# Cross-attention on one core: the first query product in two banks, the mean copied ahead of rstd's transpose, x's second half loaded in two pieces, more identity transposes

## Chip, core and metric

The kernel runs on one core of one Trainium2 chip. The metric is device time in microseconds; lower is better. Every time below is from the profile of one execution or from the list of timed runs. In the profile PE is TensorE's matmul, PEld its weight load, DVE VectorE, ACT ScalarE, POOL GpSimd and SP SyncE, whose queue issues nearly all DMAs. L317 is line 317 of the kernel.

## What is computed

Cross-attention with a LayerNorm ahead of it and a residual behind it: 8 batches of 256 rows of 1024 numbers, 32 heads of 32, keys and values both taken straight from the context (256 rows for each batch).

```python
mu = jnp.mean(hidden_states, axis=-1, keepdims=True)
var = jnp.var(hidden_states, axis=-1, keepdims=True)
x = (hidden_states - mu) * jax.lax.rsqrt(var + LN_EPS) * ln_gamma + ln_beta
Q = _split_heads(x @ Wq.T)
K = _split_heads(memory_keys)
V = _split_heads(memory_values)
scores = jnp.einsum('bhsd,bhtd->bhst', Q, K) * scale
scores = jnp.where(mask, scores, -jnp.inf)
probs = jax.nn.softmax(scores, axis=-1)
attn = jnp.einsum('bhst,bhtd->bhsd', probs, V)
out = attn @ Wout.T
return residual + out
```

## The kernel before

The work is cut into 64 steps n: batch n // 8, and within it a group of four heads, which is one 128-column chunk of the query. For each step PE makes scores (L525), VectorE adds the mask's bias and takes a minimum (L563), ScalarE takes exponents (L567), GpSimd and others normalise (L582), VectorE transposes in blocks (L588), and PE multiplies by the values (L675). Output projections of the batch before run in between (L759). The order on each engine is the order of the program text: the schedule is written out by hand, and the framework only adds the waits that tiles need. A matmul in float32 is two passes in the profile, a transpose is one.

The change touches only the start-up, which treats batch 0 apart, so that the first scores do not wait for a whole LayerNorm. x of batch 0 is loaded in halves of 128 rows: s=1 first, in two pieces of 512 columns (`load_x`, L133), then s=0 in one piece. In program order:

- `keep_busy` (L121) issues transposes of an identity tile into a PSUM tile that nobody reads.
- `ln_stats` (L231 to L239): VectorE takes statistics of rows, GpSimd raises the variance to the power -0.5 (rstd).
- `transpose_x0` (L275): PE turns raw x into PSUM, four 128x128 blocks in a bank; there are two such banks.
- `spread` (L282): PE transposes the mean, and then rstd, broadcast over columns, so that each lies along the free dimension. Both go into one PSUM tile, `stat0`.
- `keep_mean` (L285) and `keep_rstd` (L301): ScalarE copies each to SBUF.
- `centre_x0` (L288): VectorE subtracts the mean while it takes the transposed x out of PSUM.
- `gammas` (L296 on ScalarE, L298 on VectorE): each of the eight chunks is multiplied by gamma. For s=1 all eight go to ScalarE, for s=0 four each.
- `first_q` (L317): the query product of step 0 on centred x that is not yet divided by its deviation. One bank holds 128 columns for s=0, 128 for s=1, and a column that gives the bias from beta.
- `take_bias` (L329), `take_q` (L325 on VectorE, L326 on ScalarE): the bias is copied; the product is multiplied by rstd, and the bias is added.
- `scale_x0` (L304): the normalised x for the other query chunks, on VectorE and GpSimd.
- `mask_bias` (L515): VectorE turns the mask into a number to add.

Then come the scores of s=1, and a first softmax in two parts, with the second and third query products (`make_q`, L380) between them. SP's queue holds, behind the loads of x, the first query weights, the keys, the mask, and then other weights.

Of the kernel before, what the change touches and what calls it, by code (L numbers as in the profile page):

```python
# [46 lines left out]
F32 = mybir.dt.float32  # L47
# [4 lines left out]
P = 128  # L52
# [7 lines left out]
def xattn_kernel(  # L60
# [11 lines left out]
    B, S, D = x.shape  # L72
# [30 lines left out]
    ps_v = ctx.enter_context(tc.tile_pool(name="ps_v", bufs=2, space=PS))  # L103
    ps_q = ctx.enter_context(tc.tile_pool(name="ps_q", bufs=1, space=PS))
# [14 lines left out]
    def keep_busy(times):  # L119
        for _ in range(times):  # L120
            nc.tensor.transpose(busy, ident, ident)  # L121

    keep_busy(6)


    xs, ks, vs, rs = {}, {}, {}, {}
# [1 line left out]
    def load_x(b, s, h=None):  # L128

        if b not in xs:  # L130
            xs[b] = xp.tile([P, NS, D], F32, tag="x", name=f"x_{b}")
        cols = ds(0, D) if h is None else ts(h, 512)
        nc.sync.dma_start(xs[b][:, s, cols], x[b, ts(s, P), cols])  # L133
# [25 lines left out]
    wq = const.tile([P, NC, NC, P], F32, tag="wq", name="wq")  # L159
# [9 lines left out]
    def load_wq(o):  # L169
        nc.sync.dma_start(wq[:, o], wq_[o])  # L170
# [26 lines left out]
    nc.scalar.dma_start(gb, gamma_beta)  # L197
    load_x(0, 1, 0)
    load_x(0, 1, 1)
    load_x(0, 0)  # L200
    load_wq(0)
    load_k(0)
    load_mask(0)
# [42 lines left out]
    def ln_norm(b, s, engine):  # L246
# [15 lines left out]
    xcT0, xnT0 = (  # L262
        lnp.tile([P, NC, S + 1], F32, tag="xnT", name=f"x{which}T_0") for which in ("c", "n")
    )
    xnTs[0] = lambda c: xnT0[:, c, :]
    rows = sums_x.rearrange("p i c a k -> p (i c a k)")
    rows0, means0 = rows[:, :S], rows[:, ds(S, S)]
    px0, stat0 = {}, {}

    def transpose_x0(s, g):  # L270

        px0[s, g] = ps_v.tile([P, NC // 2, P], F32, tag="pv", name=f"px0_{s}_{g}")
        for i in range(NC // 2):
            chunk = xs[0][:, s, ts(NC // 2 * g + i, P)]
            nc.tensor.transpose(px0[s, g][:, i, :], chunk, ident)  # L275

    def spread(s, what):

        if what == 0:
            stat0[s] = ps_o.tile([P, 2, P], F32, tag="po", name=f"stat0_{s}")  # L280
        one = mvs[0][:, s, 0:1] if what == 0 else rstds[0][:, s : s + 1]
        nc.tensor.transpose(stat0[s][:, what, :], one.to_broadcast([P, P]), ident)  # L282

    def keep_mean(s):
        nc.scalar.copy(means0[:, ts(s, P)], stat0[s][:, 0, :])  # L285

    def centre_x0(s, g):
        nc.vector.tensor_tensor(  # L288
            xcT0[:, ts(g, NC // 2), ts(s, P)], px0[s, g],
            means0[:, ts(s, P)].unsqueeze(1).to_broadcast([P, NC // 2, P]), ALU.subtract,  # L290
        )
# [8 lines left out]
    def keep_rstd(s):  # L300
        nc.scalar.copy(rows0[:, ts(s, P)], stat0[s][:, 1, :])  # L301

    def scale_x0(s, g, engine):
        engine.tensor_tensor(  # L304
            xnT0[:, ts(g, NC // 2), ts(s, P)], xcT0[:, ts(g, NC // 2), ts(s, P)],
            rows0[:, ts(s, P)].unsqueeze(1).to_broadcast([P, NC // 2, P]), ALU.mult,
        )

    QUERY_0 = (0, 1, 2, 3, 4, 6, 5, 7)

    def first_q(s, chunks=QUERY_0):

        if s == 1 and chunks[0] == 0:
            pqs[0] = ps_q.tile([P, 512], F32, tag="pq", name="pq_0")
        cols = ds(0, P) if s == 0 else ds(P, P + 1)
        for c in chunks:
            nc.tensor.matmul(  # L317
                pqs[0][:, cols], wq[:, 0, c, :], xcT0[:, c, cols],
                start=(c == 0), stop=(c == NC - 1),
            )  # L320

    def take_q(o, bank, cols):

        to = qa[:, o, cols]
        nc.vector.tensor_tensor(to, bank[:, cols], rows0[:, cols], ALU.mult)  # L325
        nc.scalar.activation(to, to, AF.Identity, bias=qa[:, o, S : S + 1])  # L326

    def take_bias(o, bank):
        nc.scalar.copy(qa[:, o, S : S + 1], bank[:, S : S + 1])  # L329
# [39 lines left out]
    to_move, pqs = {}, {}  # L369
# [147 lines left out]
    def scores(n, part=range(NS)):  # L517
        if n not in scs:
            scs[n] = [
                ps_s.tile([P, NS, T], F32, tag="sc", name=f"sc_{n}_{j}") for j in range(NH)  # L520
            ]
        for s in part:
            for j in range(NH):
                r = slice(j * HD, (j + 1) * HD)
                nc.tensor.matmul(  # L525
                    scs[n][j][:, s, :], qa[r, n % NQ, ts(s, P)], ks[n - n % 2][r, n % 2, :],
                    start=True, stop=True,
                )
# [389 lines left out]
    def gammas(s):  # L918
        for c in QUERY_0:
            gamma_x0(s, c, nc.vector if s == 0 and c in (2, 4, 6, 7) else nc.scalar)  # L920
# [5 lines left out]
    transpose_x0(1, 0)  # L926
    keep_busy(2)
    transpose_x0(1, 1)
    keep_busy(2)
    spread(1, 0)  # L930
    keep_busy(3)
    spread(1, 1)
    keep_busy(3)
    keep_mean(1)
    keep_rstd(1)
    centre_x0(1, 0)
    centre_x0(1, 1)
    gammas(1)
# [2 lines left out]
    scale_x0(1, 1, nc.gpsimd)  # L941
    transpose_x0(0, 0)
    transpose_x0(0, 1)
    first_q(1, QUERY_0[:5])
    spread(0, 0)
    first_q(1, QUERY_0[5:])
    spread(0, 1)
    keep_mean(0)
    centre_x0(0, 0)
    centre_x0(0, 1)  # L950
    take_bias(0, pqs[0])
    gammas(0)
    keep_rstd(0)
    take_q(0, pqs[0], slice(P, S))
    scale_x0(0, 0, nc.vector)
    scale_x0(0, 1, nc.gpsimd)
    mask_bias(0)
    first_q(0)
    scores(0, (1,))
    take_q(0, pqs[0], slice(0, P))  # L960
    first = softmax_parts(0, (partial(copy_q, 1), partial(copy_q, 2)), (), (), {}, [
        partial(ln_stats, 1, 0), partial(ln_stats, 1, 1),
        partial(ln_norm, 1, 0, nc.vector),
# [34 lines left out]
    for n in range(N):  # L998
# [117 lines left out]
        if N - NQ + 2 < n < N - 1:  # L1116

            c = n - (N - NQ + 3)
# [104 lines left out]
```

## Time and profile before

| | before |
|---|---|
| median of 3 runs | 574.05 us (573.84 to 575.56) |
| profiled execution, whole | 575.86 us |
| its span, first to last instruction | 574.0 us |
| mean granted TensorE clock | 0.994 |
| busy: DVE | 468.3 us (82%) |
| busy: ACT | 426.3 us (74%) |
| moved by DMA | 119.02 MB, mean 207 GB/s |

A row of a timeline gives the start, the length from the first start to the last end, the engine, the line, the operation, what is written and read, the count, and in brackets the idle time just before it with what ended that. The chain of waits goes back from the last instruction, at each step to what released it. In rows of windows, each engine's busy time comes with the number of its instructions; the granted clock is 1.00 at full speed. A row of DMA issues ends with the median time from issue to landing.

### The profile page before, as it was taken

What the parts mean: (1) busy time and instruction counts of PE and PEld (TensorE: products, weight loads), DVE (VectorE), ACT (ScalarE), POOL (GpSimd) and SP (SyncE); (2) the same over time, 40 slices, a digit from 0 to 9 for tenths busy, and PEclk for the clock granted to TensorE, in tenths of its full rate; (3) what the DMA queues carried; (4) which work ended last, traced back from release to release, by engine and by line L of the source; (5) the groups of instructions that cost most, each with busy time, mean ns of one, the idle gap of its engine ahead of it and who ended that gap; (6) DMA issues with size and microseconds to landing.
All of it is one profiled execution on the core that took longest, in us unless ns stands there. A gap on an engine that the chain in (4) does not pass through costs nothing.

```text
span 574.0 us, 20189 instructions
## 1 busy us (share of the span) xinstructions
PE 563.7 (98%) x7246; PEld 394.3 (69%) x7246; DVE 468.3 (82%) x1718; ACT 426.3 (74%) x1478; POOL 397.9 (69%) x639
## 2 busy tenths in 40 slices
PE   6999999999999999999999999999999999999997
PEld 5777887677666776677676677667766777755544
DVE  4789889999897888988889788988878768778823
ACT  4489989998676876688577877778767766768920
POOL 3498897899875764975658675686657667448780
PEclk9799999999999999999999999999999999999999
DMA  8936477874878876886679767786667865536751
GB/s 304 397 104 197 150 207 231 265 233 122 248 254 241 236 203 188 250 245 201 175 213 284 195 199 228 221 253 199 196 175 226 243 197 142 139 104 178 218 160 73
DMA packets 47219, 119.02 MB, mean 207 GB/s; under 512 B 8976, under 2 KB 9744, under 8 KB 47120
## 3 DMA queue, kind: packets, MB, share of 16 engines
q1 hardware_dynamic: 46976, 117.74, 68.7%
q8 instruction: 57, 0.93, 0.7%
q14 instruction: 42, 0.34, 0.2%
q10 hardware_dynamic: 144, 0.01, 0.0%
HBM read 66.33 MB, written 11.53 MB: 136 GB/s over the span
## 4 chain that ended last, share of the span: by engine, by line
PE 90%; DMA 3%; DVE 3%; ACT 1%; POOL 1%; SPq 1%; issue 1%; DVEq 0%; POOLq 0%; ACTq 0%
PE po_S L759 19%; PE pq_A L486 18%; PE pv L675 11%; PE sc L525 11%; PE po_A L759 9%; PE pq L380 8%; PE pq_S L486 7%; PE po_end L826 3%; PE po_last L826 1%; DMA r<-in_x_dram 1%; ACT e L567 1%; PE pq L317 1%; DVE e L563 1%; DMA pT<-pT 1%; POOL e L582 1%
## 5 line engine op out<-in xcount | busy, mean ns | idle before, releaser
L582 POOL TENSOR_SCALAR e<-e,rden 128x256 f32<-128x256 f32 x466 | 216.7, 483 | 126.3 <-DVE rden L574 124.1
L567 ACT ACTIVATE e<-e,mn 128x256 f32<-128x256 f32 x512 | 254.1, 502 | 45.9 <-DVE mn L563 44.8
L588 DVE STREAM_TRANSPOSE pT<-e 128x512 f32<-128x512 f32 x256 | 178.9, 704 | 37.8 <-POOL e L582 32.8
L563 DVE CUSTOM_DVE_ANT_0 e<-sc,mb 128x256 f32<-128x256 f32 x512 | 185.3, 416 | 26.5 <-PE sc L525 26.3
L594 ACT COPY pc<-pT 128x512 f32<-128x512 f32 x128 | 79.0, 617 | 57.3 <-DVE pT L588 35.4
L567 ACT ACTIVATION_READ_ACCUMULATOR e<-e,mn 128x1 f32 x512 | 98.4, 192 | 0.0
L525 PEld LDWEIGHTS sc<-k,qa 32*128 32x128 f32 x1024 | 46.5, 185 | 42.1 <-issue 21.6
L525 PE MATMUL sc<-k,qa 32*128 32x256 f32 x1024 | 74.3, 403 | 0.0
L759 PE MATMUL po_S<-wo,at 128*128 128x512 f32 x152 | 74.3, 606 | 0.0
L675 PE MATMUL pv<-pT,v 64*32 64x128 f32 x4096 | 74.2, 274 | 0.0
L675 PEld LDWEIGHTS pv<-pT,v 64*32 64x32 f32 x4096 | 57.0, 105 | 22.5 <-issue 9.8
L759 PE MATMUL po_A<-wo,at 128*128 128x512 f32 x128 | 59.4, 605 | 0.0
L380 PE MATMUL pq<-xnT,wq 128*128 128x256 f32 (+1 forms) x240 | 55.6, 386 | 1.0 <-ACT qa L389 1.0
L486 PEld LDWEIGHTS pq_A<-xnT,wq 128*128 128x128 f32 x416 | 48.5, 192 | 6.2 <-issue 5.0
L380 PEld LDWEIGHTS pq<-xnT,wq 128*128 128x128 f32 x240 | 44.9, 191 | 10.0 <-issue 2.2
L759 PE MATMUL po_S<-wo,s 128*128 128x512 f32 x104 | 50.2, 607 | 0.9 <-DVE r L801 0.9
L486 PE MATMUL pq_A<-xnT,wq 128*128 128x128 f32 x416 | 48.5, 275 | 0.0
L574 DVE RECIPROCAL rden<-den 128x2 f32<-128x2 f32 x256 | 38.2, 149 | 6.6 <-ACT e L567 4.8
L563 DVE DVE_READ_ACCUMULATOR2_ANT mn<- 128x1 f32 x512 | 42.7, 83 | 0.0
L759 PEld LDWEIGHTS po_A<-wo,at 128*128 128x128 f32 x128 | 22.9, 189 | 25.7 <-issue 24.7
L759 PEld LDWEIGHTS po_S<-wo,at 128*128 128x128 f32 x152 | 25.5, 190 | 19.5 <-issue 19.5
L792 POOL TENSOR_TENSOR r<-r,p 128x512 f32<-128x512 f32 x24 | 30.6, 1277 | 4.4 <-DMA r<-in_x_dram 4.2
(109 smaller groups left out, 675.5 us busy)
## 6 DMA issues: line engine op xcount, KB each, us to landing
v<-in_kv_dram SPq DMA_DIRECT2D x32, 512.0 KB, 4.3
pT<-pT SPq DMA_DIRECT2D x128, 128.0 KB, 2.7
pT<-pc SPq DMA_DIRECT2D x128, 128.0 KB, 4.1
ring<-kept_T SPq DMA_DIRECT2D x20, 512.0 KB, 4.7
k<-in_kv_dram SPq DMA_DIRECT2D x32, 256.0 KB, 3.7
x<-in_x_dram SPq DMA_DIRECT2D x15, 512.0 KB, 6.0
r<-in_x_dram SPq DMA_DIRECT2D x28, 256.0 KB, 4.5
out_dram<-r SPq DMA_DIRECT2D x28, 256.0 KB, 4.0
```

Source lines behind the costliest of these rows:

```text
L380: nc.tensor.matmul(pqs[n], wq[:, o, c, :], xnTs[b](c), start=(c == 0), stop=(c == NC - 1),)
L486: nc.tensor.matmul(pqs[b][:, o, :], w[:, c], x_[:, c], start=begins and o + c == 0, stop=c == NK - 1, skip_group_check=True,)
L525: nc.tensor.matmul(scs[n][j][:, s, :], qa[r, n % NQ, ts(s, P)], ks[n - n % 2][r, n % 2, :], start=True, stop=True,)
L563: nc.vector.tensor_tensor_reduce(out=e[:, s, :], in0=pss[j][:, s, :], in1=mbs[n // NQ], scale=1.0, scalar=NO_SCORE, op0=ALU.add, op1=ALU.m ...
L567: nc.scalar.activation(e[:, s, :], e[:, s, :], AF.Exp, bias=mn[:, s : s + 1], scale=-1.0, accum_out=den[:, s : s + 1],)
L574: nc.vector.reciprocal(rden, dens[j])
L582: engine.tensor_scalar(es[j][:, s, :], es[j][:, s, :], rden[:, s : s + 1], 1.0, ALU.mult, ALU.mult,)
L588: nc.vector.transpose(pT[:, :, :, j, :, :].rearrange("p a i s k -> p (a i) s k"), es[j].rearrange("p s (b t) -> p b s t", t=K),)
L594: nc.scalar.copy(pc[:, :, ts(j, 2)], pT[:, 1, :, ts(j, 2)])
L675: nc.tensor.matmul(pvs[n][r][j * HD : (j + 1) * HD], vs[n - n % 2][ts(r, 2 * K), i, ds(n % 2 * P + j * HD, HD)], pT[ts(r, 2 * K), :, i, j, ...
L759: nc.tensor.matmul(po, operand(b, name)[:, c], wo[:, which, c], start=begins and c == 0, stop=c == NK - 1, skip_group_check=not begins,)
L792: nc.gpsimd.tensor_tensor(r, r, p1s[b], ALU.add)
```

## The change

- There are 14 identity transposes at the very start instead of 6. Two ahead of the first `spread` are gone; 4 instead of 3 follow the mean's and rstd's `spread` of s=1 (the latter now behind `keep_rstd`); 3 new ones stand behind `keep_rstd` of s=0.
- x's rows of s=0 are loaded in two pieces of 512 columns.
- `keep_mean` stands ahead of rstd's `spread`, for s=1 and for s=0. `keep_rstd` follows that `spread` directly; for s=0 it is ahead of the centring and the gamma products now. `take_bias` stands between the two centrings.
- Six chunks of the s=1 product stand ahead of the mean's `spread` of s=0, instead of five.
- The s=0 half of `first_q` has a bank of its own, from the pool with the two banks that `transpose_x0` used.

```diff
-    keep_busy(6)
+    keep_busy(14)
...
     load_x(0, 1, 0)
     load_x(0, 1, 1)
-    load_x(0, 0)
+    load_x(0, 0, 0)
+    load_x(0, 0, 1)
     load_wq(0)
...
-    px0, stat0 = {}, {}
+    px0, stat0, halves_q0 = {}, {}, {}
...
     def first_q(s, chunks=QUERY_0):
 
-        if s == 1 and chunks[0] == 0:
-            pqs[0] = ps_q.tile([P, 512], F32, tag="pq", name="pq_0")
+        if chunks[0] == 0:
+            pool, tag = (ps_q, "pq") if s == 1 else (ps_v, "pv")
+            halves_q0[s] = pool.tile([P, 512], F32, tag=tag, name=f"pq_0_{s}")
         cols = ds(0, P) if s == 0 else ds(P, P + 1)
         for c in chunks:
             nc.tensor.matmul(
-                pqs[0][:, cols], wq[:, 0, c, :], xcT0[:, c, cols],
+                halves_q0[s][:, cols], wq[:, 0, c, :], xcT0[:, c, cols],
                 start=(c == 0), stop=(c == NC - 1),
             )
...
     transpose_x0(1, 1)
-    keep_busy(2)
     spread(1, 0)
-    keep_busy(3)
+    keep_mean(1)
+    keep_busy(4)
     spread(1, 1)
-    keep_busy(3)
-    keep_mean(1)
     keep_rstd(1)
+    keep_busy(4)
     centre_x0(1, 0)
     centre_x0(1, 1)
...
-    first_q(1, QUERY_0[:5])
+    first_q(1, QUERY_0[:6])
     spread(0, 0)
-    first_q(1, QUERY_0[5:])
+    keep_mean(0)
+    first_q(1, QUERY_0[6:])
     spread(0, 1)
-    keep_mean(0)
+    keep_rstd(0)
+    keep_busy(3)
     centre_x0(0, 0)
+    take_bias(0, halves_q0[1])
     centre_x0(0, 1)
-    take_bias(0, pqs[0])
     gammas(0)
-    keep_rstd(0)
-    take_q(0, pqs[0], slice(P, S))
+    take_q(0, halves_q0[1], slice(P, S))
     scale_x0(0, 0, nc.vector)
     scale_x0(0, 1, nc.gpsimd)
     mask_bias(0)
     first_q(0)
     scores(0, (1,))
-    take_q(0, pqs[0], slice(0, P))
+    take_q(0, halves_q0[0], slice(0, P))
```

## The prediction

> **What bounds the kernel now.** I read the busy shares first, then the chain of waits, then windows with the granted clock, then the timelines of single engines over the first 22 us, where every edit lies.
>
> ```profile
> PE 563.7 (98%) x7246; PEld 394.3 (69%) x7246; DVE 468.3 (82%) x1718; ACT 426.3 (74%) x1478; POOL 397.9 (69%) x639
> ```
>
> TensorE (PE) fills 98% of the span, so what the change can win is a start-up that ends earlier. The chain of waits (start, length, what) shows it:
>
> ```profile
> 9.73 1.12 PE pq L317 x10
> ...
> 12.29 0.75 DVE xcT L288 x2
> ...
> 14.71 3.75 PE pq L317 x16
> 18.46 1.20 PE sc L525 x8
> 19.66 0.41 DVE e L563
> ...
> 22.81 0.35 DVE e L563
> ...
> 30.36 0.41 DVE e L563
> ...
> 36.04 3.75 PE pq L380 x16
> ```
>
> Up to 12.29 row means are made; there the centring of x's first 128 rows starts (s=0; the second 128 rows, s=1, go first). At 14.71 the sixteen passes of the last half query product run at 3.75/16 = 0.234 us each; ten passes of the same line took 1.12/10 = 0.112. From 19.66 to 36 the chain is VectorE, ScalarE and GpSimd work of the first softmax, and then PE. No load is on it there, so I let what is won at 19.66 pass to the end in full.
>
> The clock explains the 0.234. Windows (busy of PE, PEld, DVE, ACT, POOL; granted clock; DMA share; GB/s), and below them PE alone, cut at the changes of clock and halfway between:
>
> ```profile
> 13.50:14.00 0.50, 0.00 (x0) 0.00 (x0) 0.50 (x4) 0.50 (x3) 0.00 (x0) 0.83 1.05 426
> ...
> 20.50:21.00 0.50, 0.50 (x3) 0.23 (x1) 0.50 (x3) 0.50 (x3) 0.00 (x0) 0.84 1.03 410
> ```
>
> ```profile
> 0.17:3.59 3.42, 1.59 (x7) 1.00 0.48 146
> 3.59:7.00 3.41, 3.41 (x15) 1.00 0.93 308
> 7.00:10.42 3.42, 2.66 (x23) 1.00 0.92 343
> 10.42:13.83 3.41, 1.53 (x12) 1.00 1.02 415
> 13.83:17.24 3.41, 2.54 (x12) 0.50 1.03 408
> 17.24:20.66 3.42, 3.42 (x17) 0.50 1.03 410
> ```
>
> A clock of 0.83 in a slice is full speed for two thirds of it, so the clock fell at 13.83; likewise it came back at 20.66. It fell after a window with 1.53 us of work (45%), stayed low after 2.54 us (74%), rose after a full one, and was kept at 2.66 us (78%). The column says 1.00 from the start; spacing says otherwise:
>
> ```profile
> 1.35 1.54 PE L121 MATMUL busy<-ring 128*128 128x128 f32 x6 [1.35 <-POOL ring masks.py:199]
> 3.54 1.12 PE L275 MATMUL px<-ring,x 128*128 128x128 f32 x4 [0.65 <-DMA x<-in_x_dram]
> ...
> 6.58 0.42 PE L121 MATMUL busy<-ring 128*128 128x128 f32 x1
> ...
> 7.23 0.49 PE L121 MATMUL busy<-ring 128*128 128x128 f32 x3
> 10.68 0.27 PE L282 MATMUL stat<-ring,mv 128*128 128x128 f32 x1
> 11.63 0.32 PE L282 MATMUL stat<-ring,rstd 128*128 128x128 f32 x1
> 14.71 3.75 PE L317 MATMUL pq<-xcT,wq 128*128 128x128 f32 x16 [2.75 <-DVE qa L325]
> ...
> 21.15 0.71 PE L525 MATMUL sc<-k,qa 32*128 32x256 f32 x8
> 21.79 6.35 PE L380 MATMUL pq<-xnT,wq 128*128 128x257 f32 x28
> ```
>
> Six identity transposes start (1.54-0.42)/5 = 0.22 us apart, three at 7.23 (0.49-0.27)/2 = 0.11 apart: PE was at half speed until about 7.0.
>
> **The change, part by part.** *Two banks.* The row at 14.71 waited 2.75 us for VectorE to read the other half out of the shared bank. With its own bank the s=0 half waits only for its scaled chunks. The rows that feed it:
>
> ```profile
> 5.74 0.21 DVE L234 BATCH_NORM_AGGREGATE mv<-st 128x2 f32<-128x12 f32 x1
> ...
> 8.94 1.27 DVE L231 BATCH_NORM_STATS2 st<-x 128x6 f32<-128x512 f32 x2
> 10.24 0.21 DVE L234 BATCH_NORM_AGGREGATE mv<-st 128x2 f32<-128x12 f32 x1
> ...
> 13.49 0.87 DVE L298 TENSOR_SCALAR xcT<-xcT,gs 128x128 f32<-128x128 f32 x4
> 14.27 0.28 DVE L325 TENSOR_TENSOR qa<-pq,sx 128x128 f32<-128x128 f32 x1
> 14.47 0.69 DVE L304 TENSOR_TENSOR xnT<-xcT,sx 128x512 f32<-128x512 f32 x1
> 15.08 1.27 DVE L515 TENSOR_SCALAR mb<-mk 128x256 f32<-128x256 uint8 x1
> ```
>
> ```profile
> 7.43 0.27 ACT L285 COPY sx<-stat 128x128 f32<-128x128 f32 x1 [5.21 <-PE stat L282]
> ...
> 8.52 2.45 ACT L296 ACTIVATE xcT<-xcT,gs 128x128 f32<-128x128 f32 x8 [0.66 <-DVE xcT L288]
> 11.99 0.27 ACT L285 COPY sx<-stat 128x128 f32<-128x128 f32 x1 [1.02 <-PE stat L282]
> ...
> 13.01 1.28 ACT L296 ACTIVATE xcT<-xcT,gs 128x128 f32<-128x128 f32 x4 [0.70 <-DVE xcT L288]
> ```
>
> Call the start of the s=0 centring C (12.29 now). ScalarE's four gamma products end at C+2.0 (14.29), VectorE's at C+2.07 (14.36). The eight chunks come one by one from C+1.1, so PE, at 0.22 us a chunk when fast, ends about C+2.55. VectorE meanwhile takes the s=1 half, scales, and makes the mask's bias until 15.08+1.27 = 16.35, that is C+4.06. There it now waits for PE until 18.5. After the change PE is ahead: s=0 product at C+2.55, scores 0.71 later, both before C+4.06. VectorE only adds taking the s=0 half (0.2 us to the next start, 14.27 to 14.47), less 0.08 by which neighbours overlap: its first exponent starts at C+4.2. The second bank is a transpose bank that the centring has freed, so it costs nothing.
>
> *Mean ahead of rstd.* ScalarE's copy at 11.99 came right after rstd's transpose (11.63+0.32), though the mean's was over at 10.68+0.27 = 10.95. The new order frees it, and six chunks instead of five (12 passes, 1.34 us) now stand ahead of that transpose. These start when transposes of x and the first weights are there:
>
> ```profile
> 0.72 1.33 SPq L133 DMA_DIRECT2D x<-in_x_dram  x3
> 2.10 0.43 SPq L170 DMA_DIRECT2D wq<-in_wq_dram  x1
> ```
>
> ```profile
> wq<-in_wq_dram SPq DMA_DIRECT2D x1, 512.0 KB, 7.2
> ```
>
> The weights land at 2.10+7.2 = 9.3. The split of x's load puts one more issue (about 0.45 us, 1.33/3) ahead of them on SyncE's queue, and ahead of keys, mask and all later loads, for none of which an engine waits in these rows. If bytes decide, nothing moves; if issue decides, 9.75. At a DMA share of 0.92 to 0.93 I take 9.4, near the first. Then 9.4+1.34+0.27 puts the mean's transpose at 11.0; from there to centring took 12.29-11.95 = 0.34: **C = 11.35**. Bounds: 11.7 with weights at 9.75; 11.0 if they never gate and the mean itself does (it came at 10.45 and its statistics start with the centring of s=1, about 0.4 earlier below).
>
> Behind the new wait: rstd's transpose waits for the mean's copy (11.3) and ends about 11.65, its copy at 11.95; the bias and the gamma products queue behind that on ScalarE. The first gamma product would start at C+0.72 = 12.07 anyway, so 0.1 us covers it; if GpSimd made rstd half a microsecond late, C+2.55 would become C+2.95, still under C+4.06. That cover is the mask's bias on VectorE.
>
> *Transposes.* Eight more at the start: 14 x 0.213 from 1.35 ends at 4.33, past the landing of x, for which PE stops waiting at 3.54. In order behind them stand 4 of x, 2 fillers, 4 of x: 24 x 0.213 from 1.35 gives 6.46, still at half clock. The mean of s=1 is ready at 5.95 (5.74+0.21), so its transpose now waits for PE, out at 6.9, copied and centred from 7.25 instead of 7.73. Bounds: 6.6 if the clock rises by 5, 7.7 if the copy still waits for rstd. This gain of 0.5 ends at the weights' landing and adds nothing to C. Later fillers (4, 4, 3) fill idle PE time; the last three end about 12.0, before the first chunk at C+1.1 = 12.45.
>
> The clock: work on PE in the window that lost it (10.42 to 13.83) becomes the rest of the s=1 product (0.9), two transposes and fillers (0.6) and 1.4 of the s=0 product, so about 2.9 us, 85%, above the 78% at which it was kept. I take it as kept.
>
> The TensorE page of the Trainium skill (TensorE: Matmul & The Clock Gate, Part 4: PE-mode transpose) says that the full clock does not engage for transposes, which do not count as busy the same way. By that rule the new fillers buy nothing and the slower case below would hold. The trace speaks against it: the window 3.59 to 7.00 held transposes alone, and spacing halved right after it.
>
> **Sum.** First exponent at 11.35+4.2 = 15.55; from the PE and VectorE rows it starts at 19.66 now: -4.1 us, with C's bounds -3.75 to -4.45. The profiled execution took 575.86 us in all, 574.0 of it span and 1.86 around it: 575.86-4.1 = **571.8**. The median of the three runs is 574.05 (573.84 to 575.56), 1.8 below that execution. I read this as chance in where the clock falls: had it fallen at 16.5, nearly all of the s=0 product would have been fast, some 1.9 us less. So 571.8 stands against 574.05 as -2.2.
>
> **Rivals.** (a) *The 1.8 us are the profiler's.* Then all runs lose the clock as shown, and the gain comes off the median: 574.05-4.1 = 570.0. For it: two of three runs agree at 574; against: one is at 575.56.
>
> (b) *The clock drops all the same*, a window or two later. Scores take 1.20 instead of 0.71, hidden by VectorE. If low until 24.1, the 28 passes after 18.2 (21.79 now, 0.226 each) do only 13 by then, and the rest end at 27.5 against 30.36-4.1 = 26.3 where VectorE wants the next scores: 1.2 to 1.5 lost, 573.3. Against it: the 85%.
>
> (c) *The gain is eaten after 19.66.* Loads run at a share of 1.02 to 1.05 through the windows above whatever the engines do; if one gated the first softmax, time stays about 574. The chain shows no load there.
>
> (d) *Slower: PE stays cold through the start.* If transposes do not raise the clock by 9.5, the added ones only delay: centring of s=1 as above, but its rstd copy ends at 8.3, x's transposes at 10.3 (8 x 0.213), twelve passes at 13.1 (12 x 0.234), C = 13.85, s=0 product 15.1 to 18.85, where it is 18.46 now: 575.86+0.4 = 576.3, which is 2.2 over the median. For it: the fillers do push x's transposes from 3.54 to 4.33. Against it: work without a break from 1.35 to nearly 8, twice the length after which the clock rose at 7.0.
>
> **How the numbers follow.** A measurement of this kernel tells 0.3%, 1.7 us, from no change; faster means below 572.3. Forecast 0.56 (571.3 to 572.6 by itself), (a) 0.19, (b) 0.12, (c) 0.06, (d) 0.07. Faster: 0.85 of the forecast and (a), 0.67; same: the rest of it, (b) and (c), 0.26; slower 0.07. The range of 569.7 to 573.6 takes in the forecast, (a) and most of (b); (c), (d) and the rest are left out.
>
> **What would show it.** Right: granted clock 1.00 from 13.5 to 21; s=0 passes spaced 0.11 apart without a wait for VectorE's read; centring at 7.3 and 11.35; first exponent near 15.6 and the first PE stretch of L380 in the chain at 32 instead of 36. Wrong: a clock of 0.50 anywhere before 21; the mean's copy still ending behind rstd's transpose; first weights landing after 9.8; or a load in the chain between 16 and 32.

## The result and the profile after

| | before | after |
|---|---|---|
| median | 574.22 us (573.84 to 575.56, 4 runs) | 570.06 us (569.77 to 570.29, 4 runs) |
| ratio to before | | 0.9923, 95% interval 0.9906 to 0.9940 |
| span of the profiled execution | 574.0 us | 568.4 us |
| whole profiled execution | 575.86 us | 570.29 us |
| mean granted clock | 0.994 | 1.000 |

The change takes 4.2 us off the median, 5.6 us off the profiled span. What the prediction calls the first exponent, and this text after it, is VectorE's first operation of the softmax (L563 before, L565 after: the mask's bias and the minimum); ScalarE's first exponent follows it 0.47 us later in both profiles. The chain of waits after (start, length, what):

```profile
1.35 3.25 PE busy L121 x14
...
8.94 1.39 PE pq L319 x12
...
11.96 2.12 PE pq L319 x16
...
14.76 0.41 DVE e L565
...
31.14 3.75 PE pq L382 x16
```

The sixteen passes of the s=0 product take 2.12 us where they took 3.75, and begin at 11.96 instead of 14.71. The first exponent starts at 14.74 instead of 19.64; the PE stretch that was at 36.04 is at 31.14. Both moved by 4.90: the first softmax passes the gain on in full. The windows of the profile after (length, busy of PE, PEld, DVE, ACT, POOL with counts, clock, DMA share, GB/s) show PE filled and the clock at full speed where it had been 0.50:

```profile
6.80:10.20 3.40, 3.39 (x29) 2.84 (x27) 2.84 (x6) 2.82 (x10) 1.11 (x1) 1.00 0.97 377
10.20:13.60 3.40, 2.95 (x25) 2.55 (x23) 2.82 (x9) 2.23 (x8) 2.34 (x4) 1.00 1.03 419
13.60:17.00 3.40, 3.40 (x26) 2.18 (x25) 2.80 (x13) 2.19 (x8) 1.29 (x1) 1.00 1.03 405
```

Rows of its timeline, by engine, from the steps of the prediction:

```profile
6.44 0.60 PE L121 MATMUL busy<-ring 128*128 128x128 f32 x4
...
10.48 0.27 ACT L286 COPY sx<-stat 128x128 f32<-128x128 f32 x1 [0.30 <-PE stat L283]
...
10.78 1.29 DVE L289 TENSOR_TENSOR xcT<-px,sx 128x512 f32<-128x512 f32 x2 [0.93 <-ACT sx L286]
...
11.22 0.27 ACT L302 COPY sx<-stat 128x128 f32<-128x128 f32 x1 [0.47 <-PE stat L283]
...
11.96 2.12 PE L319 MATMUL pq<-xcT,wq 128*128 128x128 f32 x16 [0.45 <-ACT xcT L297]
...
12.99 1.90 POOL L305 TENSOR_TENSOR xnT<-xcT,sx 128x512 f32<-128x512 f32 x1 [1.06 <-DVE xcT L299]
...
13.56 0.29 DVE L517 TENSOR_SCALAR mb<-mk 128x256 f32<-128x256 uint8 x1
14.01 0.71 PE L527 MATMUL sc<-k,qa 32*128 32x256 f32 x8
...
14.74 0.42 DVE L565 CUSTOM_DVE_ANT_0 e<-sc,mb 128x256 f32<-128x256 f32 x1 [0.33 <-PE sc L527]
```

The mean is copied at 10.48, ahead of rstd at 11.22; the product's passes wait 0.45 us for a gamma product of ScalarE, no longer for VectorE's read; transposes are 0.11 us apart from 6.44 on ((0.60-0.27)/3).

That leaves 5.6-4.9 = 0.7 us. It lies far behind the start-up, in a wait of PE for a residual row block. The row of before, and the row of after:

```profile
179.22 1.98 PE L759 MATMUL po_S<-wo,s 128*128 128x512 f32 x4 [0.91 <-DVE r L801]
```

```profile
173.70 1.55 PE L761 MATMUL po_S<-wo,s 128*128 128x512 f32 x3 [0.25 <-DVE r L803]
```

VectorE adds to a block r there; in the chain of before a load of r from memory stands ahead of it, 6.64 us long, and in the chain of after none does. Whether the change or chance made this wait shorter is a question for the experiments.

### The profile page after: what moved, and what is told of

Same layout as the page of the kernel before. It is cut to its first block, busy times and chain, and to the rows that moved or that the text cites. A ratio compares the mean times of both kernels' runs of the same rounds, so it can differ in the third digit from the quotient of the medians.

```text
span 568.4 us, 20213 instructions
## 1 busy us (share of the span) xinstructions
PE 562.4 (99%) x7257; PEld 394.1 (69%) x7257; DVE 467.3 (82%) x1718; ACT 426.5 (75%) x1478; POOL 397.9 (70%) x639
## 4 chain that ended last, share of the span: by engine, by line
PE 91%; DVE 3%; POOL 2%; DMA 1%; ACT 1%; issue 1%; SPq 1%; DVEq 0%; ACTq 0%; POOLq 0%
PE po_S L761 20%; PE pq_A L488 18%; PE pv L677 11%; PE sc L527 11%; PE po_A L761 10%; PE pq L382 8%; PE pq_S L488 7%; PE po_end L828 3%; DVE e L565 1%; POOL e L584 1%; PE po_last L828 1%; DMA pT<-pT 1%; ACT e L569 1%; PE busy L121 1%; PE pq L319 1%
## 5 line engine op out<-in xcount | busy, mean ns | idle before, releaser
L565 DVE CUSTOM_DVE_ANT_0 e<-sc,mb 128x256 f32<-128x256 f32 x512 | 185.3, 416 | 26.1 <-PE sc L527 26.0
L565 DVE DVE_READ_ACCUMULATOR2_ANT mn<- 128x1 f32 x512 | 42.5, 83 | 0.0
```

What stands on the lines that cost most here:

```text
L565: nc.vector.tensor_tensor_reduce(out=e[:, s, :], in0=pss[j][:, s, :], in1=mbs[n // NQ], scale=1.0, scalar=NO_SCORE, op0=ALU.add, op1=ALU.m ...
```

## The experiments

Two theories. **W**: waits add up, and the clock falls only where PE idles too long. **C**: the clock is the main thing, and the parts are needed together to keep it. (C alone, without the word theory, is the start of the s=0 centring, as in the prediction.) All kernels were timed beside the kernel before. Twelve ran, in three sets of four; each set ran on a chip of its own and shared its runs of before, so medians are compared within a set, and across sets by the ratio to before.

### One part taken back

One bank again (all places of `halves_q0` as before):

```diff
...
-            halves_q0[s] = pool.tile([P, 512], F32, tag=tag, name=f"pq_0_{s}")
+            pqs[0] = ps_q.tile([P, 512], F32, tag="pq", name="pq_0")
...
```

> The changed kernel with both halves of the first query product in one bank again (everything else as changed). Theory W (the gain is a sum of waits taken off the chain, the clock is a bonus): the s=0 product starts after VectorE has read the s=1 half, at C+2.3 = 13.1 instead of 11.96, and ends at about 14.9 instead of 14.1; first exponent 15.6, time 570.06+0.85 = 570.9, clock 1.00 throughout. Theory C (the gain is mainly that the clock no longer falls in PE's gap ahead of that product): the gap grows back from 0.45 to about 1.6 us, the clock falls in most executions, the product takes over 3 us, and the time is 572.5 or more with runs that differ by 1 us.

The mean's copies back behind rstd's transpose:

```diff
     spread(1, 0)
-    keep_mean(1)
     keep_busy(4)
     spread(1, 1)
+    keep_mean(1)
     keep_rstd(1)
...
     spread(0, 0)
-    keep_mean(0)
     first_q(1, QUERY_0[6:])
     spread(0, 1)
+    keep_mean(0)
     keep_rstd(0)
```

> The changed kernel with the mean's copies behind rstd's transpose again, for s=1 and s=0. Theory W: centring of s=1 0.7 later (7.65 instead of 6.94), so the s=1 product, the mean of s=0 and then another 0.7 at its own copy: C at 12.2 instead of 10.78, time 570.06+1.4 = 571.5, clock kept. Theory C: the clock is kept as PE's gap grows by only 0.5 us, so what is lost is under 1 us (570.5 to 571.0).

The old numbers of identity transposes, at the start and at all later places:

```diff
-    keep_busy(14)
+    keep_busy(6)
...
```

> The changed kernel with the identity transposes of before (6 at the start, 2 and 2, 3 and 3, none after the s=0 rstd). Theory W: fillers buy nothing and x's first transposes start at 3.66 instead of 4.39: time 569.5 to 570.1. Theory C: the clock rises later in some executions (the stretch of unbroken work is 4 us instead of 6) and may fall again at 11; runs differ by over 1 us, median 571 to 572.

x in one load:

```diff
-    load_x(0, 0, 0)
-    load_x(0, 0, 1)
+    load_x(0, 0)
```

> The changed kernel with x's rows of s=0 in one load again. Both theories: the whole 512 KB lands near 8.0, 0.3 us after the transposes of s=0 could start (7.68), so 570.06+0.3 = 570.4 or no difference; the first weights are issued 0.47 us earlier, which shows as nothing since they are no gate in the profile of the changed kernel.

| kernel | median (lowest to highest) | ratio to before, 95% interval |
|---|---|---|
| one bank | 572.26 (571.74 to 573.61) | 0.9960 (0.9941 to 0.9979) |
| mean behind rstd | 571.88 (570.71 to 572.43) | 0.9941 (0.9918 to 0.9964) |
| old transposes | 571.08 (570.22 to 573.70) | 0.9939 (0.9922 to 0.9956) |
| one load of x | 569.64 (569.29 to 569.94) | 0.9910 (0.9890 to 0.9931) |

The bank is the clean case: its centring begins at 10.77, as after the change. From its timeline:

```profile
13.18 2.02 PE L318 MATMUL pq<-xcT,wq 128*128 128x128 f32 x16 [1.68 <-DVE qa L326]
...
15.87 0.43 DVE L564 CUSTOM_DVE_ANT_0 e<-sc,mb 128x256 f32<-128x256 f32 x1 [0.33 <-PE sc L526]
```

PE waits 1.68 us for VectorE's read, yet passes stay at 2.02/16 = 0.126 us: the clock is kept, against theory C (all five timed runs, too, show a mean clock of 1.000), and the bank alone is worth 15.87-14.74 = 1.1 us. Its time was 1.4 above what W expected; later waits of 0.36 us (at 241 us) and 0.72 us (at 244 us) for loads are in its profile, 1.1 of the 1.4. The mean's old order moves the centring to 11.97 and the first exponent to 15.94. That is 1.2 us later than in the first profile of the change, near W's 1.4, but only 0.57 later than in its second one (15.37, below). Here are the start of the s=1 product and the centring with the old order, and then in that second profile:

```profile
9.39 1.58 PE L319 MATMUL pq<-xcT,wq 128*128 128x129 f32 x12 [0.22 <-DMA wq<-in_wq_dram]
...
11.97 1.29 DVE L289 TENSOR_TENSOR xcT<-px,sx 128x512 f32<-128x512 f32 x2 [1.89 <-ACT sx L286]
```

```profile
9.38 1.58 PE L319 MATMUL pq<-xcT,wq 128*128 128x129 f32 x12
...
11.41 1.29 DVE L289 TENSOR_TENSOR xcT<-px,sx 128x512 f32<-128x512 f32 x2 [1.25 <-ACT sx L286]
```

With the s=1 product at the same time, the order is worth 11.97-11.41 = 0.56 us; the rest of the 1.2 is the product's start, 8.77 in the first profile, and with the old order it waited there for the first weights. The split of x shows no gain: without it neither the median nor the ratio is higher. The old transposes give the same first exponent in a profile as the changed kernel's second one (15.38 and 15.37). Their runs reach 573.70; all ten show a mean clock of 1.000, so no fall of it is behind that, and without a trace it stays open whether a clock that rises late, as theory C expected, or late loads are. Their ratio does not differ from the change's beyond the intervals.

### One part alone, and the changed kernel again

The second set runs the changed kernel again, and puts into the kernel before only the two banks, only the new place of the copies of mean, rstd and bias (with six chunks), or only the identity transposes, by the lines of the diff above.

> The changed kernel once more, beside the single parts on one chip. In the profiles so far the span is 553.0 to 553.8 us plus the start of the first exponent plus PE's later waits for loads (0 to 1.1 us, between 170 and 245 us). By that account: first exponent at 14.6 to 14.9, span 567.9 to 568.7, time 569.8 to 570.5.

> The kernel before with the two banks alone. Theory W (waits add up, and the clock falls only where PE idles more than some 2 us): C stays at 12.3, the s=0 product starts at C+1.2 = 13.5, PE's gap shrinks from 2.75 to 1.5 us, the clock is kept, first exponent at C+4.0 = 16.3, span 569.4 to 570.4, time 571.3 to 572.3. Theory C (the parts are needed together to keep the clock): the clock falls at the end of the window with the gap as before, the product takes 3 us and more, first exponent 18 or later, time 573 or more.

> The kernel before with the mean copied ahead of rstd's transpose alone (and six chunks ahead of it). Theory W: C at 11.4; with one bank the s=0 product starts at C+2.4 = 13.8, PE's gap is 2.0 us; with the clock kept the first exponent is at C+5.1 = 16.5 and the time 571.6 to 572.6. Theory C: the clock falls in the profile, the product takes 3.7 us, first exponent 18.3, time 573.5 or more.

> The kernel before with the identity transposes of the changed kernel alone (14 at the start, none ahead of the first spread, 4, 4, and 3 behind rstd's transpose of s=0). Theory W: C at 12.0 to 12.3, PE's gap is cut to about 2.3 us by the three; the product still waits for the shared bank; if the clock is kept, first exponent at C+5.1 = 17.3 and time 572.4 to 573.4, since half of what the fall cost comes back. Theory C with a fall all the same: first exponent 19.3, time 574.5 to 575.5.

| kernel | median (lowest to highest) | ratio to before, 95% interval | first exponent |
|---|---|---|---|
| the change, again | 569.89 (569.61 to 570.42) | 0.9933 (0.9914 to 0.9951) | 15.37 |
| banks alone | 571.89 (571.35 to 574.12) | 0.9964 (0.9950 to 0.9979) | 16.33 |
| mean alone | 572.33 (571.44 to 573.67) | 0.9971 (0.9955 to 0.9987) | 16.67 |
| transposes alone | 573.29 (572.48 to 573.69) | 0.9983 (0.9971 to 0.9994) | 17.52 |

The change's second profile has its first exponent at 15.37, later than the 14.6 to 14.9 expected, by the later s=1 product shown above. The s=0 product in the timelines of banks alone, of mean alone, of transposes alone:

```profile
13.29 2.12 PE L318 MATMUL pq<-xcT,wq 128*128 128x128 f32 x16 [1.51 <-ACT xcT L296]
```

```profile
13.98 2.02 PE L317 MATMUL pq<-xcT,wq 128*128 128x128 f32 x16 [2.01 <-DVE qa L325]
```

```profile
14.84 2.02 PE L317 MATMUL pq<-xcT,wq 128*128 128x128 f32 x16 [2.42 <-DVE qa L325]
```

In these profiles each part alone keeps the clock: after idle gaps of 1.51, 2.01 and 2.42 us the passes are fast. The times are those that W expected, all three. The other timed runs say more. Their mean clock is on record: 0.997 is what the second profile of before shows (below), where 3.41 us at half speed are its only loss.

| kernel, second set | runs with a mean clock of 0.999 or 1.000 | runs below that (0.994 to 0.997) |
|---|---|---|
| before | 5 of 25: 572.11 to 572.76 us | 20 of 25: 573.46 to 576.09 us |
| transposes alone | 3 of 10: 572.48 to 572.94 | 7 of 10: 573.09 to 573.69 |
| mean alone | 7 of 10: 571.44 to 572.75 | 3 of 10: 572.57 to 573.67 |
| banks alone | 10 of 10: 571.35 to 574.12 | none |
| the change, again | 4 of 4: 569.61 to 570.42 | none |

So the two banks alone kept the clock in every run, the mean's order in most, the transposes in three of ten, which is not clearly more than before's five of 25. Where it fell in the runs below is not traced. Neither theory holds in full: gaps of 2.42 and 2.01 us did not always keep the clock, and the parts are not all needed to keep it.

Transposes alone begin the centring at 12.42, later than the 12.29 of before, and still bring 19.26-17.52 = 1.7 us or more (19.26 is the least of before's three first exponents): that is what the clock alone is worth in a profile that keeps it. The timed runs of before agree: the five that kept it have a median of 572.57 us, those at 0.996 to 0.997 one of 574.11. The singles gain 2.9, 2.6 and 1.7 us by that measure, 7.3 together, where all of them gain 3.9 to 4.5, since each contains the clock, and the clock can be won only once. Against transposes alone at 17.52, whose s=0 product still waits for the shared bank behind the old order, the banks bring 1.2 us, the mean 0.85, 2.0 together, and the change 2.2 to 2.8: by the profiles waits come close to adding up. Medians of the runs that kept the clock do not: 0.7 for the banks and 0.6 for the mean against before, 2.7 for the change. Why is open; those runs left no trace of later waits.

### The kernel before again, no transposes, and a further step

```diff
...
-    keep_busy(14)
+    keep_busy(1)
...
```

with all other `keep_busy` calls of the start-up left out:

> The changed kernel with no identity transposes but one at the start. If the fillers buy nothing: the first transposes of x start at their landing (3.6), first exponent 14.5 to 15.4, time 569.5 to 570.5. If they carry the clock: PE's work is broken until the s=1 product, spacing of its passes stays 0.23 us, twelve passes take 2.8 instead of 1.4, C is at 12.5 to 13, the s=0 product runs partly or wholly at half speed, first exponent 16.5 to 18.5, time 571.5 to 573.7 with runs that differ by more than 1 us.

The further step puts three chunks instead of six ahead of the mean's transpose, loads x of s=0 in one piece and moves rstd's copy and the bias behind three gamma products:

```diff
-    load_x(0, 0, 0)
-    load_x(0, 0, 1)
+    load_x(0, 0)
...
-    first_q(1, QUERY_0[:6])
+    first_q(1, QUERY_0[:3])
     spread(0, 0)
     keep_mean(0)
-    first_q(1, QUERY_0[6:])
+    first_q(1, QUERY_0[3:])
     spread(0, 1)
-    keep_rstd(0)
-    keep_busy(3)
     centre_x0(0, 0)
-    take_bias(0, halves_q0[1])
     centre_x0(0, 1)
-    gammas(0)
+    gammas(0, QUERY_0[:3])
+    keep_rstd(0)
+    take_bias(0, halves_q0[1])
+    gammas(0, QUERY_0[3:])
...
```

> The changed kernel with x's s=0 rows in one load, three chunks of the s=1 product instead of six ahead of the mean's transpose, rstd's copy and the bias behind three gamma products, and no fillers behind the s=0 rstd. The mean of s=0 is ready at about 10.0 where its transpose starts at 10.8 in the last profile of the changed kernel: C at 10.75 instead of 11.41, first exponent at 14.5 to 14.9 instead of 15.37, time 569.1 to 569.5 against 569.9. If instead the s=1 product's remaining five chunks or rstd's copy become the gate: first exponent unchanged, 569.7 to 570.1.

> The kernel before, looked at again, to see where the clock falls. If the moment is chance: it falls between 12 and 16.7, or not at all, first exponent 17.3 to 19.7, and the span is 553.3 plus that plus PE's later waits for loads. If it is fixed: the fall at 13.8 and the first exponent at 19.6 again.

> The same kernel once more: a third sample of the moment at which the clock falls and of PE's wait for a load at 170 to 180 us (0.91 us in the first profile); the same account is expected to hold to 0.3 us.

Without transposes the median is 571.21 us (570.61 to 572.32), 0.9931 of before (0.9907 to 0.9955), between the two cases. Its timeline:

```profile
7.10 1.97 PE L276 MATMUL px<-ring,x 128*128 128x128 f32 x8 [0.19 <-DVE xcT L289]
8.86 2.34 PE L319 MATMUL pq<-xcT,wq 128*128 128x129 f32 x12
...
12.82 2.12 PE L319 MATMUL pq<-xcT,wq 128*128 128x128 f32 x16 [0.77 <-ACT xcT L297]
```

Twelve passes take 2.34 us against 1.58 for the same dozen in the second profile of the changed kernel, so the clock was still half for most of them; the s=0 product then is fast, and the first exponent comes at 15.61. So the fillers bring the clock some microseconds forward and the first exponent 0.2 to 0.9 us. A gain in time is not shown: the ratio of 0.9931 lies between those of the two sets of runs of the change, 0.9923 and 0.9933.

Three chunks ahead gives 569.78 us (568.92 to 570.86), 0.9907 (0.9885 to 0.9928), and the earliest first exponent, 14.36. Its interval overlaps those of the changed kernel and of the one load of x, so it is no proven step, and the time is 0.3 us above the range that was expected for it. In its timeline the s=1 product is held by the first weights:

```profile
8.98 0.91 PE L318 MATMUL pq<-xcT,wq 128*128 128x129 f32 x6 [0.21 <-DMA wq<-in_wq_dram]
```

The second and third profiles of before took 577.86 and 574.23 us. The s=0 product and PE's later waits, second profile:

```profile
15.01 3.07 PE L317 MATMUL pq<-xcT,wq 128*128 128x128 f32 x16 [2.75 <-DVE qa L325]
...
177.35 2.05 PE L486 MATMUL pq_S<-sx,ring 128*128 128x128 f32 x16 [1.22 <-DMA ring<-kept_T]
181.20 1.98 PE L759 MATMUL po_S<-wo,s 128*128 128x512 f32 x4 [1.79 <-DVE r L801]
```

Third profile, with no later wait at all:

```profile
15.05 3.03 PE L317 MATMUL pq<-xcT,wq 128*128 128x128 f32 x16 [2.75 <-DVE qa L325]
```

Both have the first exponent at 19.26 and the clock falling near 15.8, and 3.6 us between their spans. The moment of the fall moved by 2 us against the first profile: the product took 0.7 us less, its start came 0.3 later, and the first exponent changed by 0.4. What sets these two executions apart is PE's later waits, in part behind loads: 3.01 us against none. All fourteen profiles fit one account, span = 553.4 (+- 0.35) + first exponent + PE's later waits:

| profile | span | first exponent | later waits | rest |
|---|---|---|---|---|
| before | 574.0 | 19.64 | 0.91 | 553.5 |
| before, second profile | 576.0 | 19.26 | 3.01 | 553.7 |
| before, third profile | 572.4 | 19.26 | 0 | 553.1 |
| after | 568.4 | 14.74 | 0.25 | 553.4 |
| after, again | 568.6 | 15.37 | 0 | 553.2 |
| one bank | 570.7 | 15.87 | 1.08 | 553.8 |
| mean behind rstd | 569.9 | 15.94 | 0.56 | 553.4 |
| old transposes | 568.6 | 15.38 | 0 | 553.2 |
| one load of x | 568.0 | 14.95 | 0 | 553.1 |
| banks alone | 569.5 | 16.33 | 0 | 553.2 |
| mean alone | 570.6 | 16.67 | 0.55 | 553.4 |
| transposes alone | 571.0 | 17.52 | 0 | 553.5 |
| no transposes | 568.8 | 15.61 | 0 | 553.2 |
| three ahead | 567.8 | 14.36 | 0 | 553.4 |

## Why the prediction was right, and where its sizes were off

*Two banks: right.* The product waits for a gamma product, and with one bank the loss is 1.1 us. *The clock: right.* It is kept in the profile after and in a window as full as foreseen (2.95 of 3.40 us, 87%, against 85%); all eight timed runs show a mean of 1.000. What was not foreseen: the two banks would have kept it by themselves, in ten runs of ten, and five of 25 runs of before kept it without any change.

*Mean ahead of rstd: right.* I put C at 11.35 with bounds 11.0 and 11.7; the two profiles of the change have 10.78 and 11.41. Both lie 2.0 us behind the start of the s=1 product, at 8.77 and 9.38; the sum had 9.4+1.95. The lower one lies outside the bounds, because the weights had landed before 9.3 there, which I had taken as the earliest. That the weights can set this start is seen in kernels close to the change: with one bank PE waits for them until 8.75, with the old order until 9.39.

*From C to the first exponent: 4.2 foreseen, 14.74-10.78 = 3.96 measured.* Two terms were mis-sized. The mask's bias took 0.29 us instead of the 1.27 copied from the row of before, so that PE's scores, not VectorE, come last. And the s=0 product ended at C+3.30 (14.08), not C+2.55: by the prediction's own terms eight chunks at 0.22 from C+1.1 make C+2.86, and its sixteen passes took 2.12 us. With both, the scores behind that later product set 3.96; that 4.2 is so near is in part luck. Banks alone still had 1.27, and 16.33-12.11 = 4.22 there, as the prediction had it.

*The base: wrong in the main.* I took the 1.8 us between the profiled execution and the median for chance in the clock, and so took the profile's time for the base. The further profiles show that a fall 2 us later is worth 0.4 us and that later waits make more, 0.91 against none; 0.3 to 0.5 us stay open. Chance does decide whether the clock falls at all, but a run that keeps it takes about 572.6, and the median of 574.05 is close to the third profile (574.23), which lost it. So the sum carried over 0.91 us of waiting that the profile after has as 0.25: 4.1+0.81 (first exponent at 14.74 instead of 15.55)+0.66 = 5.6, the measured difference of spans. By this 571.8 was 1.5 too high for the profiled execution (570.29) and 1.7 for the median. That the median still lies in the range, 0.4 above its lower end, is in part luck: 571.3 to 572.6, the forecast by itself, does not hold it, and the range went lower only for rival (a).

*Rivals.* (a) gave the measured number for a wrong reason: what lies around the span is 570.29-568.4 = 1.9 us after, as before, and the timed run of 569.77 us has a span of 567.9, so nothing shows that the profiled execution bears a cost of its own. Its condition, that the runs of before lose the clock, holds for 20 of 25. (b) did not occur in the change; with the mean's order alone or the transposes alone the mean clock suggests that it did in three and in seven of ten runs. (c) fell: 4.90 us at 15 are 4.90 us at 31. (d), PE cold through the start, fell too: even without transposes the clock rose before the s=0 product.

*The Trainium skill's rule on transposes* (TensorE: Matmul & The Clock Gate, Part 4: PE-mode transpose), by which they do not engage the full clock, is not borne out: transposes alone preceded the spacing of 0.11 us at 6.44, and with nearly all fillers gone, spacing of 0.22 us or more lasted past 8.86.

*Open:* whether the change itself shortens the later waits. Two profiles of it show 0.25 and 0 us, three of before 0.91, 3.01 and 0; eight timed runs of the change lie within 0.8 us, while the 20 of before that lost the clock spread over 2.6 us and the five that kept it over 0.7. No run held the late loads fixed.

## What to carry to other kernels

Ask of each part of a start-up change whether it also cures what another part cures: here three single parts each had the clock back in their profile, so their single gains add up to 7.3 us where the whole brings 3.9 to 4.5. One profile does not show how often: the mean clock of the timed runs told that the banks kept it in ten runs of ten and the transposes in three. Take a second and third profile of the kernel before, before a difference between one profile and the median is given a cause. Filling idle time of the engine whose clock can fall, and cutting the wait itself, are two cures for one loss; here cutting the wait was the surer one, and it gave its own length on top.

## What the hardware showed that was not expected

The falls of the clock fit how full a stretch of 3.41 us was, better than the length of a gap alone. The low clock lasted 3.41 us in the second profile of before and 6.83, twice that, in the first, where it fell at 13.83, inside the gap; in the second it fell at 15.76, with the gap over since 15.01. PE's busy time in such stretches: the second profile of before, cut at the changes of clock, then transposes alone. There the clock did not change, so the cuts are an estimate, in steps of 3.41 from 6.91, where the spacing of transposes halves.

```profile
12.35:15.76 3.41, 0.75 (x7) 1.00 1.03 416
15.76:19.17 3.41, 3.41 (x20) 0.50 1.03 404
```

```profile
10.32:13.74 3.42, 2.09 (x17) 1.00 1.03 420
13.74:17.15 3.41, 2.31 (x24) 1.00 1.03 405
```

It fell after 0.75 us of work in 3.41 (and after 1.53 in the first profile), and was kept after 2.09, 61%, with a gap of 2.42 us. That seven other runs of the same kernel, and 20 of 25 of before, show a lower mean clock would fit a gap that falls differently across the stretches from run to run; no trace of those runs shows it. The same page of the Trainium skill (TensorE: Matmul & The Clock Gate, Why this matters for your kernels) warns of idle gaps over some 3 us; here the 2.75 us of before were enough in all three profiles.

The mask's bias, one VectorE instruction of unchanged shape, takes 0.29 us in some kernels and 1.27 in others, always beside a GpSimd multiply that has just started. Banks alone:

```profile
14.34 1.69 POOL L304 TENSOR_TENSOR xnT<-xcT,sx 128x512 f32<-128x512 f32 x1 [1.80 <-ACT sx L301]
14.91 1.27 DVE L516 TENSOR_SCALAR mb<-mk 128x256 f32<-128x256 uint8 x1
```

There GpSimd takes 1.69 us and VectorE 1.27, and VectorE ends 0.15 us behind GpSimd; after the change they take 1.90 and 0.29, and VectorE ends 1.04 us ahead. One of the two seems to wait for the other. In all fourteen profiles the 1.27 goes with a GpSimd multiply released by ScalarE's copy of rstd (five: the three profiles of before, banks alone, transposes alone), the 0.29 with one released by VectorE (nine). Why that decides was not tested by itself.
